# Four mask chunks at once, applied in the transform, and a layer-0 scan without products on GpSimd

## The chip, the cores and the metric

One Trainium2 chip, one of its cores. The metric is the device time of the one launch in microseconds: the median over several runs, and beside it one execution that the hardware profiler recorded. In the profile the engines are PE (TensorE's matmuls), PEld (TensorE's weight loads), DVE (VectorE), ACT (ScalarE), POOL (GpSimd) and SP (SyncE, which here only issues DMAs). POOL also issues DMAs: all gathers by index are issued there.

## The reference

Four samples x of 96 channels and 128 x 128 pixels in float32 go through four layers, each with a group norm `_gn` (32 groups) ahead of it and a residual sum behind it. Cut to what the change touches:

```
x = x + L0(_gn(x))
x = x + L1(_gn(x))
x = x + L2(_gn(x))
x = x + L3(_gn(x))
```

Layer 0 convolves, and then runs a selective scan over the 16,384 pixels, once forward and once backward (K = 2, one state per channel):

```
delta = softplus(dts + dt_proj_b)
dA = exp(delta * A)
dBu = (delta * xs) * Bs
h = dA * h + dBu
ys = h * Cs + Ds * xs
y = ys[forward] + reversed(ys[backward])
y = (y - mean_c(y)) * rsqrt(var_c(y) + 1e-05)
y = y * out_norm_w + out_norm_b
y = y * silu(z)
out = out_proj_w @ y
```

Layer 1 is a mix of spatial, fractional-Fourier and Fourier branches with gates. Layer 2 is a deformable 3 x 3 convolution: an offset for each pixel and tap, a bilinear gather, a weighting, a product with the weights. Layer 3 masks the pixels by their likeness to the centre pixel, takes a two-dimensional cosine transform, runs a scan in each quadrant, and transforms back:

```
center = x[:, :, H // 2, W // 2]
sim = sum_c(x * center) / (|center| * |x| + 1e-06)
x = x * (sim >= 0.7)
xd = Mh @ x @ Mw^T
...
return Mh^T @ (xd + scans) @ Mw
```

## The kernel before

**Tiles.** A plane of 96 channels x 16,384 pixels lies in device memory. Most work is done in NCH = 32 chunks of [96 channels, 512 pixels]. The transforms work in 24 pieces of [128 rows, 4 channels, 128 columns]. In layer 2 a row of the image is 128 pixels on partitions: per tap one gather of [128, 4 x 96] values (tile l_g; 1,152 gathers per sample), then four weighings by bilinear weights (two on ACT, two scalar_tensor_tensor on DVE, tiles l_sm and l_part), a sum, transposes on PE (l_pt), a copy (l_sT), and the product with the layer's weights (l_pc).

**Stages of one sample.** `front` (L635) runs layer 0 (L645), layer 1 (L822) and the offsets of layer 2 (L1212). `back` (L1375) runs the gather of layer 2 (L1386), `layer3_head` (L1493, the mask), and `transform` (L1565, the forward cosine transform). `layer3` (L1604) runs the four quadrant scans, and `inverse` (L1579) the transform back with the residual.

**Lanes.** The front of sample b+1 and the back of sample b are issued as two lanes of one program, and the inverse of sample b-1 runs inside that front, beside layer 0's convolution. So: the front of sample 0 alone, three mixed epochs, each followed by `layer3` of one sample alone, then the back of sample 3 beside the inverse of sample 2, `layer3` of sample 3, and the last inverse. The change touches nothing of `layer3`.

**The order.** Every instruction of both lanes is recorded (class `Program`, L237) and issued by a list scheduler (`issue`, L388). It gives each operation a cost from a table (`cost`, L359) and a due time: `measure` (L282) plans each lane by itself, and the time between two starts is stretched by `pace`, which the code of a stage can set. Each lane's due times are scaled to the same span, so that both lanes end together. An operation that is ready and has the earliest due time goes first. For a DMA the cost table has two numbers, the time on its issuing engine and its share of a common DMA resource ("landing"). The scan of layer 0 sets the pace to 0.1 (L724); layer 1 sets it back to 1. The engines then run their queues strictly in that order. Since all instructions pass through one helper, the profile puts nearly all of them on L65 and SP's DMAs on L412; groups are told apart by tile names.

**Layer 0's scan** (`scan(k, n)`, L728 to L818): 64 calls per sample, k = 0 forward and k = 1 backward. Loads of l_uc (and, in the second half, l_x, l_z and l_part); pd on PE; |.|, relu, exp, ln on ACT; dl = relu + ln on DVE; pB on PE; dA = exp on ACT; du = uc * pB on DVE, then du = du * dl on POOL; the scan h on DVE; its last column copied by ACT (l_e) as the start of the next call; pC on PE; h = h * pC in place on DVE. In the first half of each direction h goes to memory as part_d. In the second half both directions are summed and centred by three matmuls into pm; ACT squares and copies it (l_ct); cavg gives the variance; ct is multiplied by the inverse root on DVE, scaled and shifted by ACT (Identity with v[7] and v[8]), multiplied by sz on DVE, projected (po) and added to l_x.

**The mask** (`layer3_head`). The square of the reference's division is avoided: with q = 0.49 |center|^2, the mask is sqrt(q |x|^2) + 0.7e-6 <= x . center. Each of 32 chunks: load l_hx, normalise on DVE, square on ACT, two 96-column matmuls (pn: |x|^2 by a matrix of ones, pd: by the centre repeated in 96 columns), Sqrt on ACT, comparison on DVE, product with the normalised chunk on POOL, store of 192 KB to m_d. A float32 matmul appears in the profile as two passes.

**The transform** (`transform2`, L1536). Each of 24 pieces: load from m_d as [128, 4, 128], four matmuls (p1), copy on ACT, four matmuls (p2), copy on DVE (l_xo), store to xd_d. `inverse` uses the same function.

**Buffers.** In mixed epochs the back has two PSUM buffers of tag "t" and one of tag "pc"; alone it has five of "t" (`room`, L1378).

Of the kernel before, what the change touches and what calls it, by code (L numbers as in the profile page):

```python
# [236 lines left out]
class Program:  # L237
# [121 lines left out]
    def cost(self, engine, name, out, ins):  # L359
# [5 lines left out]
        if name == "indirect_dma_start":  # L365
            return 1.25, 0.3
# [145 lines left out]
class Net:  # L512
# [132 lines left out]
    def layer0(self, xin, T, beside):  # L645
# [3 lines left out]
        with self.program.pool(name="l0w", bufs=1) as wp, self.program.pool(name="l0p", bufs=1, space=PSUM) as ps:  # L649
# [74 lines left out]
            self.program.pace = 0.1  # L724
            with self.program.pool(name="l0b", bufs=3) as wb:
                edges = [None, None]

                def scan(k, n):  # L728
# [16 lines left out]
                    tmp = wb.tile([C, CH], F32, name="l0_tmp", tag="tmp")  # L745
# [14 lines left out]
                    nc.gpsimd.tensor_tensor(du, du, dl, ALU.mult)  # L760
                    yield
                    h = wb.tile([C, CH], F32, name="l0_h", tag="h", bufs=5)
                    prev = edges[k]
                    if k == 0:
                        nc.vector.tensor_tensor_scan(
                            h, dA, du, 0.0 if prev is None else prev, ALU.mult, ALU.add
                        )
                        edge = h[:, CH - 1 : CH]
                    else:
                        nc.vector.tensor_tensor_scan(  # L770
                            h[:, ::-1], dA[:, ::-1], du[:, ::-1],
                            0.0 if prev is None else prev, ALU.mult, ALU.add,
                        )
                        edge = h[:, 0:1]
                    edges[k] = wb.tile([C, 1], F32, name="l0_e", tag="edge", bufs=6)
                    nc.scalar.copy(edges[k], edge)
# [5 lines left out]
                    nc.vector.tensor_tensor(h, h, pC, ALU.mult)  # L782
                    if not second:
                        nc.sync.dma_start(out=part_d[:, s], in_=h)
                        yield
                        return
# [6 lines left out]
                    nc.tensor.matmul(out=pm, lhsT=center[:, 0, :], rhs=h, start=False, stop=True)  # L793
# [4 lines left out]
                    nc.scalar.copy(ct, pm)  # L798
# [9 lines left out]
                    nc.scalar.activation(ct, ct, AF.Identity, bias=v[:, 8:9], scale=v[:, 7:8])  # L808
                    yield
                    nc.vector.tensor_tensor(ct, ct, sz, ALU.mult)  # L810
# [564 lines left out]
    def back(self, T, alone=False):  # L1375
# [3 lines left out]
        with self.program.pool("l2v", 1) as wp, self.program.pool("l2b", 2) as wb, self.program.pool(  # L1379
            "l2q", room[0], PSUM  # L1380
        ) as ps:
            yield from self.gather(T, wp, wb, ps, *room[1:])
            yield from self.layer3_head(T, wp, wb, ps)
            yield from self.transform(T, wp, wb, ps)

    def gather(self, T, wp, wb, ps, rows, sums, kept, lag, slack):  # L1386
# [60 lines left out]
        def finish(p, c):  # L1447
            g, h = divmod(p, 2)
            w, v = work[g], units.pop((p, c))
            if h == 0 and c == 0:  # L1450
                w.pc = ps.tile([C, CH], F32, name="l2_pc", tag="pc", bufs=1)
# [41 lines left out]
    def layer3_head(self, T, wp, wb, ps):  # L1493

        nc = self.nc
        T.m = self.plane("m_d")
# [4 lines left out]
        cc = wp.tile([C, C], F32, name="l3_cc")  # L1501
        nc.vector.tensor_copy(cc, xm.to_broadcast([C, C]))
        cs = wp.tile([C, 2], F32, name="l3_cs")
        nc.scalar.activation(cs[:, 0:1], xm, AF.Square)
        yield
        pn = ps.tile([128, CH], F32, name="l3_pn", tag="t")
        nc.tensor.matmul(out=pn[:C, 0:1], lhsT=self.ones, rhs=cs[:, 0:1], start=True, stop=True)
        nc.vector.tensor_scalar_mul(cs[:, 1:2], pn[:C, 0:1], 0.49)
        yield

        def piece(t):
            s = slice(t * CH, (t + 1) * CH)
            x = wb.tile([C, CH], F32, name="l3_hx", tag="hx", bufs=5)
            nc.sync.dma_start(out=x, in_=T.x3[:, s])
            yield
            yield
            nc.vector.tensor_scalar(x, x, scale, shift, ALU.mult, ALU.add)
            sq = wb.tile([C, CH], F32, name="l3_sq", tag="sq", bufs=3)
            nc.scalar.activation(sq, x, AF.Square)
            yield  # L1520
            pn = ps.tile([C, CH], F32, name="l3_pn", tag="t")
            nc.tensor.matmul(out=pn, lhsT=self.ones, rhs=sq, start=True, stop=True)
            pd = ps.tile([C, CH], F32, name="l3_pd", tag="t")
            nc.tensor.matmul(out=pd, lhsT=cc, rhs=x, start=True, stop=True)
            yield
            nc.scalar.activation(sq, pn, AF.Sqrt, scale=cs[:, 1:2])
            yield
            nc.vector.scalar_tensor_tensor(sq, sq, 0.7e-6, pd, ALU.add, ALU.is_le)
            yield
            nc.gpsimd.tensor_tensor(x, x, sq, ALU.mult)  # L1530
            nc.sync.dma_start(out=T.m[:, s], in_=x)
            yield

        yield from staggered((piece(t) for t in range(NCH)), 2)

    def transform2(self, src, mat, ps, wt, tags, extra, done):  # L1536
# [4 lines left out]
        def piece(cb):  # L1541
            cs = slice(4 * cb, 4 * cb + 4)
            xt = wt.tile([128, 4, W], F32, name="t2_in", tag=tags[0][0], bufs=tags[0][1])
            nc.sync.dma_start(out=xt, in_=s3[:, cs, :])
            more = extra(cs)
# [10 lines left out]
            p2 = ps.tile([128, 4, 128], F32, name="t2_p2", tag=tags[3], bufs=tags[4])  # L1556
# [8 lines left out]
    def transform(self, T, wp, wb, ps):  # L1565
# [10 lines left out]
        tags = ("hx", 5), ("sq", 3), "t", "t", None  # L1576
        yield from self.transform2(T.m, dctT, ps, wb, tags, lambda cs: None, put)

    def inverse(self, T, out, ps, wt):  # L1579
# [17 lines left out]
        tags = ("in", 4), ("mid", 2), "c", "c", 2  # L1597
# [787 lines left out]
```

## Time and profile before

| what | us |
|---|---|
| median of 3 runs (15122.8 to 15134.95) | 15123.15 |
| profiled execution, its own time | 15123.18 |
| its span, first to last instruction | 15121.3 |
| front of sample 0 alone | 0 to 1304 |
| mixed epochs: gather of the first to end of the last, lengths | 2110, 2135, 2130 |
| four layer-3 scans (first to last matmul l_py), each | 1404 to 1408 |
| last back: gathers | 11949.5 to 13414.2 |
| last back: mask (l_hx), transform (l_xo) | 13429 to 13511, 13527 to 13592 |

The mean granted TensorE clock is 0.898 of full speed. Two lines of the page's busy tenths in 40 slices (each digit is a slice of 378 us; 9 is 90% or more) show that PE and DVE change places as the fuller engine:

```profile
PE   7897887879997978888999688888999744459998
DVE  3626686668998587677999578666999765548997
```

The stretches in which both lines stand at 8 and 9 are the layer-3 scans. Between them lie the mixed epochs, with PE mostly at 7 to 8 and DVE at 5 to 8: there no engine is full all the time, and a stretch has to be read by itself. A time there is read from a table of windows (busy time of each engine between two points), and the cost of one instruction from the groups (mean ns after the comma).

### The profile page before, as it was taken

The page shows a single profiled execution, that of the slowest core. Times are in us where ns is not written, and L with a number is a line of the kernel's source. Part 1 is how long each engine was busy: PE and PEld are TensorE (multiplying, and loading weights), DVE is VectorE, ACT ScalarE, POOL GpSimd, SP SyncE. Part 2 cuts the span into 40 slices and gives each one's busy share as a digit, 9 for nine tenths or more (in the row PEclk, how much of TensorE's full clock was granted, in tenths as well). Part 3 has the DMA queues.
Part 4 walks back from the last instruction along what each step waited for, and adds up shares of the span by engine and source line. Part 5 has one row for each costly group of instructions (what it writes and reads, how often), then busy time and mean ns, then how long its engine had stood idle before and what let it go on. Part 6 is the DMA issues. An engine that isn't in the chain of part 4 may idle for free. (4 is left out here: it accounts for less than half of the span.)

```text
span 15121.3 us, 175326 instructions
## 1 busy us (share of the span) xinstructions
PE 12434.4 (82%) x48096; PEld 5808.6 (38%) x48096; DVE 11294.8 (75%) x21519; ACT 8958.7 (59%) x21605; POOL 10394.8 (69%) x7936
## 2 busy tenths in 40 slices
PE   7897887879997978888999688888999744459998
PEld 3353334343332334444333233534333422233334
DVE  3626686668998587677999578666999765548997
ACT  3614685556664576555666467555666465546664
POOL 2104747748998765765999674773999877748997
PEclk9997898989998989989999899998999855579999
DMA  4546659766666767876666765976666755556666
GB/s 115 143 127 201 191 167 253 229 201 183 187 197 193 234 181 213 239 218 185 194 189 194 218 208 167 259 227 192 194 188 194 216 171 165 167 149 181 189 197 192
DMA packets 1326732, 2914.81 MB, mean 193 GB/s; under 512 B 282864, under 2 KB 768944, under 8 KB 1211440
## 3 DMA queue, kind: packets, MB, share of 16 engines
q1 hardware_dynamic: 1027376, 1997.21, 45.8%
q0 software_dynamic: 298368, 906.38, 20.2%
q8 instruction: 382, 6.26, 0.2%
q14 instruction: 606, 4.96, 0.1%
HBM read 2455.28 MB, written 447.48 MB: 192 GB/s over the span
## 5 line engine op out<-in xcount | busy, mean ns | idle before, releaser
L65 POOL DMA_INDIRECT l_g<-quad_d,l_i x4608 | 4648.1, 1009 | 2541.0 <-issue 1319.5
L65 POOL TENSOR_TENSOR l_hc<-l_h,l_cl 128x1024 f32<-128x1024 f32 x1536 | 3609.7, 2362 | 287.9 <-DVE l_h L65 259.0
L65 PE MATMUL l_py<-l_hc,ident 128*128 128x512 f32 x6144 | 3068.4, 610 | 185.9 <-POOL l_hc L65 182.4
L65 DVE TENSOR_TENSOR_SCAN l_h<-l_dA,l_carry,l_dB 128x512 f32<-128x512 f32 x2304 | 2863.6, 1266 | 1.7
L65 DVE SCALAR_TENSOR_TENSOR l_sm<-l_g,l_v,l_sm 128x96 f32<-128x96 f32 x4608 | 1491.3, 324 | 1137.8 <-ACT l_sm L65 1041.2
L65 ACT ACTIVATE l_dA<-l_dl,l_al 128x512 f32<-128x512 f32 x2304 | 1637.4, 718 | 1111.6 <-DVE l_h L65 1102.3
L65 ACT ACTIVATE l_sm<-l_g,l_v 128x96 f32<-128x96 f32 x4608 | 1677.6, 369 | 731.2 <-DMA l_g<-quad_d,l_i 634.4
L65 ACT ACTIVATE l_part<-l_g,l_v 128x96 f32<-128x96 f32 x4608 | 1654.8, 363 | 234.9 <-DVE l_sm L65 234.4
L65 PEld LDWEIGHTS l_py<-l_hc,ident 128*128 128x128 f32 x6144 | 1133.6, 192 | 1352.9 <-issue 829.2
L65 PE MATMUL l_pc<-l_sT,l_wk 128*96 128x256 f32 (+1 forms) x3584 | 1244.2, 471 | 418.8 <-ACT l_sT L65 418.1
L65 PE MATMUL l_pt<-ident,l_sm 128*128 128x128 f32 (+1 forms) x3584 | 798.3, 327 | 909.4 <-DVE l_sm L65 827.9
L65 DVE TENSOR_TENSOR l_dB<-l_du,l_pB 128x512 f32<-128x512 f32 x2304 | 1493.9, 678 | 49.5 <-POOL l_du L65 26.7
L65 DVE SCALAR_TENSOR_TENSOR l_part<-l_g,l_v,l_part 128x96 f32<-128x96 f32 x4608 | 1485.8, 323 | 36.3 <-ACT l_part L65 35.6
L65 PE MATMUL l_pB<-l_bc,pick 128*128 128x512 f32 x2304 | 1399.8, 635 | 135.4 <-DVE l_dB L65 121.5
L65 POOL TENSOR_TENSOR l_dP<-l_du,l_cl 128x512 f32<-128x512 f32 x768 | 978.6, 1274 | 101.0 <-DMA l_cl<-bc_d 74.6
L65 PEld LDWEIGHTS l_pt<-ident,l_sm 128*128 128x128 f32 (+1 forms) x3584 | 522.9, 165 | 1317.5 <-DVE l_sm L65 922.1
L65 DVE TENSOR_TENSOR_SCAN l_h<-l_dQ,l_carry,l_dP 128x512 f32<-128x512 f32 x768 | 971.8, 1265 | 58.3 <-POOL l_dP L65 54.9
L65 PEld LDWEIGHTS l_pc<-l_sT,l_wk 128*96 128x96 f32 (+1 forms) x3584 | 646.5, 200 | 944.3 <-ACT l_sT L65 513.2
L65 PE MATMUL l_pc<-rows,l_wc 96*32 96x508 f32 (+3 forms) x6912 | 919.6, 601 | 2.4 <-DVE rows L65 2.4
L65 POOL TENSOR_TENSOR l_du<-l_du,l_dl 96x512 f32<-96x512 f32 x256 | 339.6, 1327 | 834.1 <-DVE l_dl L65 487.1
L65 ACT COPY l_sT<-l_pt 128x512 f32<-128x512 f32 (+1 forms) x1024 | 520.8, 522 | 656.1 <-PE l_pt L65 654.0
L65 PE MATMUL l_p<-rows,l_c 96*32 96x508 f32 (+3 forms) x6912 | 823.1, 598 | 83.9 <-issue 46.7
(265 smaller groups left out, 19771.8 us busy)
## 6 DMA issues: line engine op xcount, KB each, us to landing
l_cl<-bc_d SPq DMA_DIRECT2D x512, 1280.0 KB
l_cl<-bc_d SPq DMA_DIRECT2D x512, 640.0 KB
quad_d<-l_qt SPq DMA_DIRECT2D x124, 768.0 KB
l_g<-quad_d,l_i POOLq DMA_INDIRECT x4608
x<-l_x SPq DMA_DIRECT2D x352, 192.0 KB
l_uc<-u_d SPq DMA_DIRECT2D x256, 192.0 KB
l_x<-x SPq DMA_DIRECT2D x224, 192.0 KB
l_xs<-x SPq DMA_DIRECT2D x116, 256.0 KB
```

The lines of the kernel that those rows point to most:

```text
L65: ins = op(*args, **kw).ins
```

## The change

1. The scheduler's cost table gives a gather a landing of 0.66 instead of 0.3, and the scan of layer 0 a pace of 0.3 instead of 0.1.
2. Layer 0's scan: du * dl on DVE instead of POOL; the copy of the last column falls away, since h is no longer overwritten (the product goes to a tile l_y) and the next call reads h's last column; h has four buffers instead of five, tmp two instead of three; the copy of pm applies the scale v[7], the Identity operation falls away, and the shift v[8] is added in the product with sz (scalar_tensor_tensor).
3. The mask: groups of four chunks. Each chunk's two matmuls have 32 output columns at partitions 32j to 32j+31 of shared PSUM tiles, so that one Sqrt and one comparison serve four chunks at [128, 512]. One row of each 32 is stored (2 KB) to mask_d, which is loaded once as a [128, 128] image. pd has the "pc" buffer. Small tiles give scale and shift as rows (by_channel) for the transform's layout.
4. The transform loads x3 instead of m_d, and normalises each of four channels on DVE ([128, 128]) and masks the piece on POOL ([128, 512], the mask broadcast). p2 has the "pc" buffer in mixed epochs.

```diff
@@ -363,7 +363,7 @@
...
         if name == "indirect_dma_start":
-            return 1.25, 0.3
+            return 1.25, 0.66
         if engine == "PE":
@@ -721,7 +721,7 @@
...
-            self.program.pace = 0.1
+            self.program.pace = .3
             with self.program.pool(name="l0b", bufs=3) as wb:
@@ -742,7 +742,7 @@
...
                     dl = wb.tile([C, CH], F32, name="l0_dl", tag="dl")
-                    tmp = wb.tile([C, CH], F32, name="l0_tmp", tag="tmp")
+                    tmp = wb.tile([C, CH], F32, name="l0_tmp", tag="tmp", bufs=2)
                     bias = v[:, 1 + k : 2 + k]
@@ -757,31 +757,30 @@
...
                     yield
-                    nc.gpsimd.tensor_tensor(du, du, dl, ALU.mult)
-                    yield
-                    h = wb.tile([C, CH], F32, name="l0_h", tag="h", bufs=5)
+                    nc.vector.tensor_tensor(du, du, dl, ALU.mult)
+                    yield
+                    h = wb.tile([C, CH], F32, name="l0_h", tag="h", bufs=4)
                     prev = edges[k]
...
                         )
-                        edge = h[:, CH - 1 : CH]
+                        edges[k] = h[:, CH - 1 : CH]
                     else:
...
                         )
-                        edge = h[:, 0:1]
-                    edges[k] = wb.tile([C, 1], F32, name="l0_e", tag="edge", bufs=6)
-                    nc.scalar.copy(edges[k], edge)
+                        edges[k] = h[:, 0:1]
                     if second:
...
                     yield
-                    nc.vector.tensor_tensor(h, h, pC, ALU.mult)
+                    y = wb.tile([C, CH], F32, name="l0_y", tag="y")
+                    nc.vector.tensor_tensor(y, h, pC, ALU.mult)
                     if not second:
-                        nc.sync.dma_start(out=part_d[:, s], in_=h)
+                        nc.sync.dma_start(out=part_d[:, s], in_=y)
                         yield
@@ -790,12 +789,12 @@
...
                     nc.tensor.matmul(out=pm, lhsT=center[:, 0, :], rhs=part, start=False, stop=False)
-                    nc.tensor.matmul(out=pm, lhsT=center[:, 0, :], rhs=h, start=False, stop=True)
+                    nc.tensor.matmul(out=pm, lhsT=center[:, 0, :], rhs=y, start=False, stop=True)
                     yield
...
                     nc.scalar.activation(sq, pm, AF.Square)
-                    nc.scalar.copy(ct, pm)
+                    nc.scalar.activation(ct, pm, AF.Copy, scale=v[:, 7:8])
                     yield
@@ -805,9 +804,7 @@
...
                     yield
-                    nc.scalar.activation(ct, ct, AF.Identity, bias=v[:, 8:9], scale=v[:, 7:8])
-                    yield
-                    nc.vector.tensor_tensor(ct, ct, sz, ALU.mult)
+                    nc.vector.scalar_tensor_tensor(ct, ct, v[:, 8:9], sz, ALU.add, ALU.mult)
                     yield
@@ -1380,8 +1377,8 @@
...
             yield from self.gather(T, wp, wb, ps, *room[1:])
-            yield from self.layer3_head(T, wp, wb, ps)
-            yield from self.transform(T, wp, wb, ps)
+            yield from self.layer3_head(T, wp, wb, ps, room[2])
+            yield from self.transform(T, wp, wb, ps, alone)
@@ -1448,7 +1445,7 @@
...
             if h == 0 and c == 0:
-                w.pc = ps.tile([C, CH], F32, name="l2_pc", tag="pc", bufs=1)
+                w.pc = ps.tile([128, CH], F32, name="l2_pc", tag="pc", bufs=1)[:C]
             for i, k in enumerate(v.ks):
@@ -1490,50 +1487,64 @@
...
-    def layer3_head(self, T, wp, wb, ps):
+    def layer3_head(self, T, wp, wb, ps, sums):
         nc = self.nc
-        T.m = self.plane("m_d")
+        mask_d = self.plane("mask_d", (NCH // 4, 4 * CH))
         mid = (H // 2) * W + W // 2
...
         nc.vector.tensor_scalar(xm, xm, scale, shift, ALU.mult, ALU.add)
-        cc = wp.tile([C, C], F32, name="l3_cc")
-        nc.vector.tensor_copy(cc, xm.to_broadcast([C, C]))
-        cs = wp.tile([C, 2], F32, name="l3_cs")
-        nc.scalar.activation(cs[:, 0:1], xm, AF.Square)
+        cc = wp.tile([C, 32], F32, name="l3_cc")
+        nc.vector.tensor_copy(cc, xm.to_broadcast([C, 32]))
+        cs = wp.tile([128, 2], F32, name="l3_cs")
+        nc.scalar.activation(cs[:C, 0:1], xm, AF.Square)
+        wide = wb.tile([C, 4, 128], F32, name="l3_wide", tag="hx", bufs=5)
+        for k, v in enumerate((scale, shift)):
+            nc.vector.tensor_copy(wide[:, k, :], v.to_broadcast([C, 128]))
+        nc.vector.memset(wide[:, 2, :], 1.0)
         yield
         pn = ps.tile([128, CH], F32, name="l3_pn", tag="t")
-        nc.tensor.matmul(out=pn[:C, 0:1], lhsT=self.ones, rhs=cs[:, 0:1], start=True, stop=True)
-        nc.vector.tensor_scalar_mul(cs[:, 1:2], pn[:C, 0:1], 0.49)
+        nc.tensor.matmul(out=pn[:, 0:1], lhsT=wide[:, 2, :], rhs=cs[:C, 0:1], start=True, stop=True)
+        nc.vector.tensor_scalar_mul(cs[:, 1:2], pn[:, 0:1], 0.49)
+        pq = ps.tile([128, CH], F32, name="l3_pq", tag="t")
+        for k in range(2):
+            nc.tensor.matmul(
+                out=pq[:, C * k : C * k + C], lhsT=wide[:, k, :], rhs=self.ident[:C, :C], start=True, stop=True
+            )
+        keep = wb.tile([128, 9, C], F32, name="l3_keep", tag="sm", bufs=sums).rearrange("p k c -> p (k c)")
+        T.by_channel, T.mask = keep[:, : 2 * C], keep[:, 2 * C : 2 * C + W]
+        nc.vector.tensor_copy(T.by_channel, pq[:, : 2 * C])
         yield
-        def piece(t):
-            s = slice(t * CH, (t + 1) * CH)
-            x = wb.tile([C, CH], F32, name="l3_hx", tag="hx", bufs=5)
-            nc.sync.dma_start(out=x, in_=T.x3[:, s])
-            yield
-            yield
-            nc.vector.tensor_scalar(x, x, scale, shift, ALU.mult, ALU.add)
-            sq = wb.tile([C, CH], F32, name="l3_sq", tag="sq", bufs=3)
-            nc.scalar.activation(sq, x, AF.Square)
-            yield
-            pn = ps.tile([C, CH], F32, name="l3_pn", tag="t")
-            nc.tensor.matmul(out=pn, lhsT=self.ones, rhs=sq, start=True, stop=True)
-            pd = ps.tile([C, CH], F32, name="l3_pd", tag="t")
-            nc.tensor.matmul(out=pd, lhsT=cc, rhs=x, start=True, stop=True)
-            yield
-            nc.scalar.activation(sq, pn, AF.Sqrt, scale=cs[:, 1:2])
-            yield
-            nc.vector.scalar_tensor_tensor(sq, sq, 0.7e-6, pd, ALU.add, ALU.is_le)
-            yield
-            nc.gpsimd.tensor_tensor(x, x, sq, ALU.mult)
-            nc.sync.dma_start(out=T.m[:, s], in_=x)
-            yield
-        yield from staggered((piece(t) for t in range(NCH)), 2)
-    def transform2(self, src, mat, ps, wt, tags, extra, done):
+        def group(g):
+            pn = ps.tile([128, CH], F32, name="l3_pn", tag="t")
+            pd = ps.tile([128, CH], F32, name="l3_pd", tag="pc", bufs=1)
+            for j in range(4):
+                x = wb.tile([C, CH], F32, name="l3_hx", tag="hx", bufs=5)
+                nc.sync.dma_start(out=x, in_=T.x3[:, (4 * g + j) * CH : (4 * g + j + 1) * CH])
+                yield
+                nc.vector.tensor_scalar(x, x, scale, shift, ALU.mult, ALU.add)
+                sq = wb.tile([C, CH], F32, name="l3_sq", tag="sq", bufs=3)
+                nc.scalar.activation(sq, x, AF.Square)
+                at = slice(32 * j, 32 * j + 32)
+                nc.tensor.matmul(out=pn[at], lhsT=self.ones[:, :32], rhs=sq, start=True, stop=True)
+                nc.tensor.matmul(out=pd[at], lhsT=cc, rhs=x, start=True, stop=True)
+                yield
+            m = wb.tile([128, CH], F32, name="l3_m", tag="l2_x", bufs=3)
+            nc.scalar.activation(m, pn, AF.Sqrt, scale=cs[:, 1:2])
+            nc.vector.scalar_tensor_tensor(m, m, 0.7e-6, pd, ALU.add, ALU.is_le)
+            for j in range(4):
+                nc.sync.dma_start(
+                    out=mask_d[g : g + 1, j * CH : (j + 1) * CH], in_=m[32 * j : 32 * j + 1]
+                )
+            yield
+        for g in range(NCH // 4):
+            yield from group(g)
+        nc.sync.dma_start(out=T.mask, in_=mask_d.rearrange("g (r w) -> (g r) w", w=W))
+    def transform2(self, src, mat, ps, wt, tags, extra, done, prepare=None):
@@ -1542,6 +1553,8 @@
...
             nc.sync.dma_start(out=xt, in_=s3[:, cs, :])
+            if prepare is not None:
+                prepare(cs, xt)
             more = extra(cs)
@@ -1553,7 +1566,7 @@
...
             yield
-            p2 = ps.tile([128, 4, 128], F32, name="t2_p2", tag=tags[3], bufs=tags[4])
+            p2 = ps.tile([128, 4, 128], F32, name="t2_p2", tag=tags[3], bufs=tags[5])
             for j in range(4):
@@ -1562,7 +1575,7 @@
...
-    def transform(self, T, wp, wb, ps):
+    def transform(self, T, wp, wb, ps, alone):
@@ -1573,8 +1586,15 @@
...
-        tags = ("hx", 5), ("sq", 3), "t", "t", None
-        yield from self.transform2(T.m, dctT, ps, wb, tags, lambda cs: None, put)
+        def prepare(cs, xt):
+            for j in range(4):
+                scale = T.by_channel[:, cs.start + j : cs.start + j + 1]
+                shift = T.by_channel[:, C + cs.start + j : C + cs.start + j + 1]
+                nc.vector.tensor_scalar(xt[:, j, :], xt[:, j, :], scale, shift, ALU.mult, ALU.add)
+            nc.gpsimd.tensor_tensor(xt, xt, T.mask.unsqueeze(1).to_broadcast([128, 4, W]), ALU.mult)
+        tags = ("hx", 5), ("sq", 3), "t", *(("t", None, None) if alone else ("pc", None, 1))
+        yield from self.transform2(T.x3, dctT, ps, wb, tags, lambda cs: None, put, prepare)
@@ -1594,7 +1614,7 @@
...
-        tags = ("in", 4), ("mid", 2), "c", "c", 2
+        tags = ("in", 4), ("mid", 2), "c", "c", 2, 2
         yield from self.transform2(T.yd_d, dct, ps, wt, tags, take, put_out)
```

## The prediction

> **What bounds the kernel now.** First the busy shares, which name no engine:
>
> ```profile
> PE 12434.4 (82%) x48096; PEld 5808.6 (38%) x48096; DVE 11294.8 (75%) x21519; ACT 8958.7 (59%) x21605; POOL 10394.8 (69%) x7936
> ```
>
> So the span must be cut into stages, by the first and last instruction of tiles that only one stage has. It falls into the front of sample 0 alone (0 to 1304 us), three mixed epochs of about 2120 us (back of one sample beside the front of the next), the last back alone (11949 to 13628), and four layer-3 scans of about 1405 us, whose code does not change. Second, the table by stretch. Rows one to five are the second mixed epoch (layer 0's convolution, its scan, layer 1, the last convolution, the offsets with mask and transform); six is the first half of sample 0's scan; seven and eight are mask and transform of the last back. Columns: stretch, length, busy time of PE, weight load, DVE, ACT, POOL, granted clock, DMA share, GB/s.
>
> ```profile
> 4848.00:5358.00 510.00, 409.17 (x2836) 183.38 (x2837) 277.63 (x863) 267.27 (x838) 365.88 (x367) 0.89 0.82 242
> 5358.00:5815.00 457.00, 381.83 (x921) 147.88 (x919) 416.26 (x721) 385.63 (x870) 238.48 (x196) 0.92 0.52 157
> 5815.00:6259.00 444.00, 362.60 (x1657) 235.37 (x1658) 292.34 (x936) 245.38 (x810) 308.99 (x303) 0.88 0.92 252
> 6259.00:6542.00 283.00, 269.14 (x2012) 101.09 (x2011) 172.70 (x545) 143.19 (x486) 211.81 (x215) 0.97 0.76 224
> 6542.00:6971.00 429.00, 341.40 (x1408) 196.19 (x1406) 306.25 (x826) 247.10 (x659) 177.76 (x164) 0.85 0.67 207
> 268.00:430.00 162.00, 133.94 (x279) 44.03 (x280) 136.86 (x168) 134.61 (x258) 52.08 (x39) 0.96 0.36 107
> ```
> ```profile
> 13429.00:13521.00 92.00, 70.78 (x130) 22.52 (x130) 42.56 (x67) 39.52 (x65) 44.76 (x32) 0.85 0.44 129
> 13521.00:13628.00 107.00, 75.33 (x437) 55.22 (x437) 24.49 (x56) 29.02 (x47) 3.21 (x4) 0.89 0.55 148
> ```
>
> Each stage has another limit: the scan DVE (416 of 457 us, 91%), layer 1 the DMA engines (0.92), the last convolution PE (95%), the fifth stretch PE (80%) with DVE close (71%). Third, the groups of instructions inside the scan stage (mean after the comma), and of the whole page the convolution with 32 output columns:
>
> ```profile
> L65 POOL DMA_INDIRECT l_g<-quad_d,l_i x132 | 153.2, 1160 | 82.0 <-issue 31.4 <-DVE l_sm L65 30.0 <-ACT l_dl L65 10.1
> L65 POOL TENSOR_TENSOR l_du<-l_du,l_dl 96x512 f32<-96x512 f32 x64 | 85.8, 1342 | 136.8 <-DVE l_dl L65 110.5 <-DVE l_du L65 25.6
> L65 DVE SCALAR_TENSOR_TENSOR l_sm<-l_g,l_v,l_sm 128x96 f32<-128x96 f32 x137 | 60.0, 444 | 6.9 <-ACT l_sm L65 6.2 <-DMA l_g<-quad_d,l_i 0.5
> L65 DVE TENSOR_TENSOR l_dl<-l_dl,l_tmp 96x512 f32<-96x512 f32 x64 | 56.7, 888 | 2.7 <-ACT l_tmp L65 2.3
> L65 DVE TENSOR_TENSOR l_h<-l_h,l_pC 96x512 f32<-96x512 f32 x64 | 43.1, 674 | 1.1 <-ACT l_e L65 0.7 <-PE l_pC L65 0.3
> L65 ACT ACTIVATE l_ct<-l_ct,l_v 96x512 f32<-96x512 f32 x32 | 26.0, 811 | 13.4 <-DVE l_ct L65 13.3
> ```
> ```profile
> L65 PE MATMUL l_pc<-rows,l_wc 96*32 96x508 f32 (+3 forms) x6912 | 919.6, 601 | 2.4 <-DVE rows L65 2.4
> ```
>
> To be seen: l_dl and l_sm take 888 and 444 ns here, though the median of l_sm in the same stage is 308 and an l_dl that meets no POOL product takes about 682. DVE is held up by POOL's own product.
>
> **The change, part by part.** The sum starts from the profiled execution: 15123.18 us, 1.9 over its span and within 0.1 of the 15123.15 median.
>
> *Where gathers go.* The planner's two new numbers (landing 0.66, pace 0.3) add no instruction; they only reorder. The compiled order of both kernels shows how many weighing operations (two per gather) stand on DVE beside each front stage, per mixed epoch: convolution 688 to 694, scan 274 to 324, layer 1 603 to 678, last convolution 413 to 383, offsets 326 to 225. So +3, +25, +37, -15 and -50 gathers.
>
> *Scan, mixed epochs.* DVE gets 64 products that were POOL's. An added one is like l_h<-l_h,l_pC, 0.674 us: +43 us. What they stop doing to DVE: 137 x (444-308) + 137 x (423-308) = 34 us on l_sm and l_part, and 64 x (888-682) = 13 on l_dl; the instructions that truly overlap a POOL product carry 30 and 14, and I take 44. The last product of the gate becomes a scalar_tensor_tensor, 32 x (0.740-0.674) = +2. The 25 gathers bring 25 x 2 x 0.308 = 15 and their share of the final additions, 25/4.57 x 0.683 = 4. DVE: 416+43-44+2+19 = 436. At today's 91% that is 479 us, at 95% it is 459; I take 465, +8 (0 to +23), since the chain loses a step. It loses POOL's 1.34 us and its wait (137 us idle), the edge copy (64 x 0.184 on ACT) and the affine (32 x 0.811): ACT falls by 38 and regains 25 x 2 x 0.365 = 18. Next in the chain l_h then waits for DVE's own queue. POOL falls from 238 to 238-86+25x1.05 = 179, so its queue has room. The fourth h buffer and second tmp buffer cost nothing while DVE sets the pace. If the 44 us do not come back, the stage goes to (436+44)/0.91 = 527.
>
> The Trainium skill, "SBUF — State Buffer" (section "SBUF: two separate sides"), says a DVE operation with two SBUF inputs and GpSimd lock each other out of a shared port for a whole instruction. The row: gathers here take 1160 ns on average, median 1050, against 967 in the last back. By the rule 64 new two-input products would block POOL for up to 43 us per epoch; by the row the excess over the quiet stretch is 0.19 us each; either way POOL at 179 of 465 us hides it, so it enters no sum.
>
> *Scan, sample 0 alone.* First half: DVE is 137 of 162 us; 32 products add 21.6 and the quieter l_dl (1.09 to 0.68 us here) gives back 13: +8 against a removed POOL step. Second half: PE is busy in 169.7 of 170 us, which covers everything. I take 0 (-5 to +10).
>
> *Layer 1, mixed.* 37 more gathers. A gather's share of the DMA engines is 0.202 x 15121/4608 = 0.66 us; at 0.92 busy, +27. Bounds: PE cost alone (transposes and products, (798.3+1244.2)/4608 = 0.44 us each by the page's l_pt and l_pc groups) +16; POOL's whole 1.2 us, +45.
>
> *Convolutions, mixed.* +3 gathers x 0.66/0.82 = +2. In the last, 15 fewer x 0.44/0.95 = -7 (0 to -14).
>
> *Mask, transform and offsets, mixed (fifth stretch).* PE loses 50 x 0.44 = 22 us, and the mask's 128 passes at 0.63 us become 128 passes of 32 columns. The convolution row shows what four neighbours on different columns do: 919.6/6912 = 0.13 us each of elapsed time, though one lasts 0.60. Here the order mixes pd and pn of one chunk (same columns), so I take half of 78 us, -37. PE: 341 to 282; at 80% that is 354 us, -75. DVE loses 50 x 2 x 0.308 + 8 of gathers, 24 x 0.68 of comparisons, and gains 96 tensor_scalars of 128x128, no row; nearest are a 96x96 copy, 0.205, and 128x96 weighing, 0.308; I take 0.28: +27. DVE: 306-39-16+27 = 278, at 71% 390 us, -39. POOL loses 32 x 1.4 = 45 and gains 24 masked products of 512 columns at about 1.35, 32. I take -50 (-20 to -75), between the two.
>
> SP's queue changes: 32 stores of 192 KB go, 32 stores of one row (2 KB) and one load come, 0.30 us of issue each, so SP is even; 6.3 MB of writes per sample vanish. What waits behind a mask store on SP is the load of the next group's chunks, at most one Sqrt and one comparison (1.4 us).
>
> Per mixed epoch: +2+8+27-7-50 = -20; three give -60.
>
> *Last back alone.* The mask's 32 chunks take 92 us, PE 71: two products of two passes each, 2.78 of 2.84 us per chunk. After, per group of four: 16 passes between 0.13 (2.1 us) and 0.63 (10 us), I take 0.32, 5.2; then Sqrt 0.68 and comparison 0.68 before pd's single buffer is free, and 0.5 for handoffs (estimated from the 0.1 to 0.2 us between dependent instructions): 7 us. Eight groups 56, the new small tiles +3: -33 (-50 to +0). The turn to the transform stays a store that must land before a load (5.3 us from the last m_d issue to the first product now). The transform keeps its loop of two products and a copy, 2.78 us a piece; its new work (4 x 0.28 + 1.35 on DVE and POOL) lies ahead of it under five buffers, costing nothing; without that cover 24 x 2.5 = 60 us.
>
> The skill speaks against the 2 KB stores: "DMA: Bandwidth & Descriptors", Rules for kernel authors, wants small transfers coalesced, and "Anatomy of one DMA — SWDGE (gpsimd) path" puts about 2 us fixed on each. By that the last four stores cost an estimated 2 us once; if nothing overlapped, 64 us. The trace has no such store.
>
> Total: 0 - 60 - 33 = -93: **15,030 us**.
>
> **Rivals.**
> *Larger gain.* PE is the true limit of the epoch: fifth stretch -75, last convolution -14, layer 1 only +16, scan 0, convolution +2: -71 x 3 - 50 = -263, 14,860. For: PE leads in four of five rows. Against: DVE at 91% and DMA at 0.92 exactly where gathers are added.
> *Nothing.* The gathers are only moved: what the offsets lose, scan and layer 1 take (fifth stretch -39, scan +23, layer 1 +27, -5: +6 x 3), the last head alone gains 33: 15,108; with a head that saves only 10, 15,131. For: each moved gather costs about the same in either place.
> *Slower: the scan's DVE gets no relief.* If gathers, which also slow DVE's operations, keep l_sm and l_dl long, the stage is 527 us, +70: per epoch +2+70+27-7-50 = +42, x 3 - 33 = +93, 15,216. It decides from +39 on that stage (496 us). For: DVE is already at 91%. Against: l_sm's median of 308 with gathers running all along.
> *Not what it says:* the scan might get no more gathers; the order shows 274 to 324, so I give that nothing.
>
> **How the numbers follow.** Forecast 0.46, larger gain 0.20, nothing 0.17, slower 0.17. A measurement tells 0.2% (30 us) from no change. Nearly all of the first two is below 15,093: faster 0.66, same 0.17, slower 0.17. The forecast's own range is 14,950 to 15,095. To hold 8 in 10 I leave out the lower end of the larger gain (0.09) and the upper end of the slower case (0.11): 14,880 to 15,190.
>
> **What would show it.** In after's scan stage l_dl near 0.68 and l_sm near 0.31 us, DVE above 91%, the stage 457 to 480 us; layer 1 about 470 at DMA 0.92 or more; the fifth stretch near 380; the last mask near 59 us with 32-column passes overlapping; transform 67. Wrong if l_sm stays above 0.4, or if a mask group takes 10 us, or if the transform waits for DVE or POOL.

## The result, and the profile after

The changed kernel takes 15220.18 us (median of 6 runs, 15186.34 to 15243.47), the kernel before beside it 15122.97: a ratio of 1.0065, 95% interval 1.0051 to 1.0079. It is slower by about 97 us where 93 us less was forecast. The profiled execution took 15215.73 us, its span is 15213.7.

The busy shares of the changed kernel, first line of its page:

```profile
PE 12702.1 (83%) x48112; PEld 5786.9 (38%) x48112; DVE 11312.4 (74%) x22079; ACT 8797.0 (58%) x21125; POOL 10025.4 (66%) x7648
```

PE is busy for 268 us more, though the mask's matmuls became cheaper. Where that lies, the table by stretch tells: the second mixed epoch again (layer 0's convolution, scan, layer 1, last convolution, and offsets with mask and transform), then mask and transform of the last back. Columns as in the prediction: stretch, length, busy time of PE, weight load, DVE, ACT, POOL, clock, DMA share, GB/s.

```profile
4838.00:5372.00 534.00, 471.43 (x2846) 185.41 (x2847) 282.46 (x872) 272.67 (x848) 369.57 (x372) 0.93 0.79 232
5372.00:5815.00 443.00, 381.78 (x959) 152.33 (x957) 423.11 (x843) 375.32 (x834) 171.59 (x158) 0.93 0.59 174
5815.00:6310.00 495.00, 362.96 (x1699) 243.89 (x1702) 312.42 (x1018) 272.19 (x903) 362.07 (x348) 0.86 0.88 244
6310.00:6663.00 353.00, 346.93 (x1987) 108.77 (x1979) 166.86 (x521) 131.03 (x443) 193.42 (x194) 0.99 0.58 170
6663.00:7029.00 366.00, 309.03 (x1350) 174.67 (x1348) 273.55 (x778) 198.14 (x517) 113.94 (x104) 0.85 0.63 198
...
13562.00:13605.00 43.00, 35.34 (x134) 10.91 (x134) 21.95 (x50) 23.62 (x40) 0.00 (x0) 0.92 0.45 139
13605.00:13720.00 115.00, 77.63 (x439) 56.81 (x436) 54.09 (x149) 29.29 (x47) 33.59 (x28) 0.87 0.50 137
```

Against the rows of before: +24, -14, +51, +70, -63. The last convolution is the surprise. It has fewer gathers beside it than before (194 instead of 215), fewer instructions on PE (1987 instead of 2012), and PE is busy for 347 us instead of 269, in 98% of the stretch. The three mixed epochs take 2107, 2199 and 2207 us instead of 2110, 2135 and 2130, and the last back 1637 instead of 1678: -3, +64, +77 and -41, together the +97. (The first epoch's last convolution also gets 94 us longer, but what follows it there gets 118 shorter.)

Two groups of the changed kernel's page say which instructions of PE became dear: l_pc<-rows,l_wc is layer 0's convolution, l_p<-rows,l_c the last one. Both are 3 x 3 convolutions, and each of the nine positions (a tap) is four matmuls with 32 output columns, eight passes. The third line is l_p before (the other stands in the prediction):

```profile
L65 PE MATMUL l_p<-rows,l_c 96*32 96x508 f32 (+3 forms) x6912 | 1058.7, 598 | 49.0 <-DMA rows<-cat_d 43.7
...
L65 PE MATMUL l_pc<-rows,l_wc 96*32 96x508 f32 (+2 forms) x6912 | 1038.3, 595 | 2.7 <-DVE rows L65 2.7
```
```profile
L65 PE MATMUL l_p<-rows,l_c 96*32 96x508 f32 (+3 forms) x6912 | 823.1, 598 | 83.9 <-issue 46.7
```

One pass lasts about 598 ns before and after. The elapsed time that all of them cover, the number after the bar, rises from 823.1 + 919.6 = 1743 us to 1058.7 + 1038.3 = 2097. They overlap less. The timeline of PE in the last convolution shows why (start, length, engine, instruction, how many in a row). First the kernel before, then the changed one:

```profile
6381.82 1.04 PE L65 MATMUL l_p<-rows,l_c 96*32 96x512 f32 x8
6382.80 0.76 PE L65 MATMUL l_pt<-ident,l_sm 128*128 128x128 f32 x5
6383.49 1.90 PE L65 MATMUL l_p<-rows,l_c 96*32 96x508 f32 x13
```
```profile
6453.32 1.04 PE L65 MATMUL l_p<-rows,l_c 96*32 96x512 f32 x2
6454.30 0.67 PE L65 MATMUL l_pc<-l_sT,l_wk 128*96 128x256 f32 x2
6454.90 1.04 PE L65 MATMUL l_p<-rows,l_c 96*32 96x508 f32 x2
6455.87 0.44 PE L65 MATMUL l_pt<-ident,l_sm 128*128 128x128 f32 x2
6456.24 1.04 PE L65 MATMUL l_p<-rows,l_c 96*32 96x508 f32 x2
```

Eight passes, the four matmuls of a tap on their four groups of columns, take 1.04 us together. Two passes, one matmul of the four, take 1.04 us alone. In both traces the unbroken runs of l_p take (medians) 1.04 to 1.06 us for 2 to 8 passes, 1.90 to 1.92 for 10 to 16, 2.75 to 2.78 for 18 to 24 and 3.60 to 3.62 for 26 to 32: about 0.2 us per run and 0.85 for every eight passes begun. The changed order puts transposes (l_pt) and products (l_pc<-l_sT,l_wk) of the gather lane between the four. Such a break stands within a tap 258 times before and 603 times after, in the compiled orders and in the traces alike (the expectations call breaks "broken taps"; they fall on 246 and 381 of the 1,728 taps; l_pz of layer 0, also 32 columns wide, isn't counted). That is 354 us more for 345 more breaks, 1.03 us each.

### The profile page after: what moved, and what is told of

Its sections match the earlier page's. It is cut to its first block, busy times and chain, and to the rows that moved or that the text cites. A ratio compares the mean times of both kernels' runs of the same rounds, so it can differ in the third digit from the quotient of the medians.

```text
span 15213.7 us, 174518 instructions
## 1 busy us (share of the span) xinstructions
PE 12702.1 (83%) x48112; PEld 5786.9 (38%) x48112; DVE 11312.4 (74%) x22079; ACT 8797.0 (58%) x21125; POOL 10025.4 (66%) x7648
## 5 line engine op out<-in xcount | busy, mean ns | idle before, releaser
L65 DVE SCALAR_TENSOR_TENSOR l_sm<-l_g,l_v,l_sm 128x96 f32<-128x96 f32 x4608 | 1426.5, 313 | 1283.3 <-ACT l_sm L65 1238.4
L65 ACT ACTIVATE l_sm<-l_g,l_v 128x96 f32<-128x96 f32 x4608 | 1619.5, 369 | 782.4 <-DMA l_g<-quad_d,l_i 699.1
L65 ACT ACTIVATE l_part<-l_g,l_v 128x96 f32<-128x96 f32 x4608 | 1607.9, 364 | 415.1 <-DVE l_sm L65 412.4
L65 DVE SCALAR_TENSOR_TENSOR l_part<-l_g,l_v,l_part 128x96 f32<-128x96 f32 x4608 | 1430.6, 314 | 169.0 <-ACT l_part L65 168.7
L65 PE MATMUL l_p<-rows,l_c 96*32 96x508 f32 (+3 forms) x6912 | 1058.7, 598 | 49.0 <-DMA rows<-cat_d 43.7
L65 PE MATMUL l_pc<-rows,l_wc 96*32 96x508 f32 (+2 forms) x6912 | 1038.3, 595 | 2.7 <-DVE rows L65 2.7
L65 PEld LDWEIGHTS l_pB<-l_bc,pick 128*128 128x128 f32 x2304 | 437.9, 190 | 1062.6 <-DVE l_dB L65 839.7
```

The lines of the kernel that those rows point to most:

```text
L65: ins = op(*args, **kw).ins
```

## The experiments

**Four runs for three theories.** A: the broken taps cost the time. B: layer 1 is held by the DMA engines and got more gathers. C (the forecast's rival): DVE gets no relief in the scan. The kernel before took 15143.33 us (13 runs) beside these.

The first undoes one number:

```diff
-            return 1.25, 0.66
+            return 1.25, 0.3
```

> The changed kernel with one number undone: a gather's landing in the scheduler's table is 0.3 again instead of 0.66. Theory A (broken taps): the changed order puts gather products of the other lane between the four 32-column matmuls of a convolution tap, 603 times against 258 before, and the elapsed PE time of these matmuls rose from 1743 to 2097 us, about 1.03 us for each break. This kernel's order has 293 breaks: up to 310 x 1.03 = 319 us less, so 14900 to 14980 us, and the last convolution of a mixed epoch back from 353 to about 285 us. Theory B (layer 1 is held by DMA and given more gathers): here layer 1 gets 601 weighings instead of 678, and only its 51 us per epoch come back: 15070 to 15130, last convolution still near 350. Theory C (the scan's DVE gets no relief): no change, 15220.

Measured: 14861.31 us, ratio 0.9813 (0.9797 to 0.9829), a little below A's range. The landing number alone is worth 2.5% of the time. Layer 1 and the last convolution of its second mixed epoch:

```profile
5689.00:6126.00 437.00, 355.42 (x1648) 235.55 (x1650) 288.98 (x931) 243.64 (x802) 307.06 (x299) 0.89 0.93 252
6126.00:6405.00 279.00, 266.20 (x2014) 100.25 (x2007) 171.69 (x541) 141.47 (x483) 211.46 (x214) 0.97 0.78 228
```

Both came back, so A and B are not told apart yet; C is out. The second keeps the landing of 0.66 and only forbids broken taps:

```diff
+        op.narrow = name == "matmul" and out.rows[1] - out.rows[0] <= 32 and out.at[0].size > 256
...
-                starts.append((start, op.key + late, op.lane, len(starts), op))
+                first = 1.0 if op.narrow and self.quad % 4 else 0.0
+                starts.append((start, op.key + late - first, op.lane, len(starts), op))
...
+            self.quad += op.narrow
```

> The changed kernel with landing 0.66 as it is, and one rule more in the scheduler: once the first of four 32-column matmuls is issued on PE, the other three go ahead of anything else. The order has 0 breaks and gives the stages the same gathers as the changed kernel (338, 679, 378 and 225 weighings in scan, layer 1, last convolution and offsets of the second mixed epoch, against 324, 678, 383 and 225). Theory A: up to 603 x 1.03 = 621 us less PE time, of which DVE and DMA will let only a part through; 14700 to 14950, the last convolution at 270 us or less. Theory B: layer 1 keeps its 679 weighings, so 15180 or more. Theory C: no change, 15220.

Measured: 14897.53 us, ratio 0.9835 (0.9818 to 0.9851). The same two stretches:

```profile
5717.00:6210.00 493.00, 368.14 (x1713) 247.39 (x1717) 314.62 (x1019) 271.99 (x903) 356.59 (x343) 0.86 0.88 243
6210.00:6475.00 265.00, 254.48 (x1981) 99.14 (x1974) 166.19 (x517) 130.89 (x443) 183.89 (x182) 0.98 0.74 216
```

The last convolution falls from 353 to 265 us and layer 0's convolution from 534 to 497, while layer 1 stays at 493. With the gathers in nearly the same places the rule alone is worth 2.3% (ratio 0.9835 against 1.0065): A is what made the kernel slow. The rule also holds for the mask's 32-column matmuls, but the last back's mask takes 43 us with it and without it. B's stretch is longer too, but 51 us there stand against 63 us less in the offsets.

The third puts the landing of 0.66 alone into the kernel before; the edit is the first one reversed.

> The kernel before with one number changed: landing 0.66. No instruction differs. Breaks 258 to 460. Theory A: up to 202 x 1.03 = 208 us more, 15220 to 15330, with the last convolution above 330 us. Theory B: 670 weighings in layer 1 instead of 603 cost about 50 us per epoch there, and the last convolution stays near 285: about 15200 or less, if the offsets give back. Theory C: no change, 15123.

Measured: 15338.64 us, ratio 1.0129 (1.0112 to 1.0146), just above A's range. No instruction differs from before, and:

```profile
5834.00:6326.00 492.00, 365.65 (x1690) 244.33 (x1694) 311.19 (x1008) 270.19 (x900) 350.72 (x336) 0.87 0.89 239
6326.00:6713.00 387.00, 376.65 (x2049) 108.63 (x2042) 186.02 (x576) 144.95 (x489) 225.83 (x227) 0.98 0.61 173
```

Layer 1 gets 48 us longer, the last convolution 104. The fourth puts the rule of the second into the kernel before.

> The kernel before with the rule that keeps the four 32-column matmuls of a tap together: 0 breaks instead of 258, gathers where they were (284, 603, 413, 326). Theory A: up to 258 x 1.03 = 266 us less, 14880 to 15030. Theories B and C: no change, 15123.

Measured: 15118.7 us, ratio 0.9986 (0.9976 to 0.9996). Here A's number missed twice. 258 breaks are gone and only 135 us of elapsed time with them (1743 to 1608), 0.52 us per break: counted in the traces, the runs of l_p begin 916 groups of eight passes before and 864 with the rule, 52 fewer for 115 broken taps (in the changed kernel they begin 1,131). And the run gains 0.14%. The last convolution, and POOL in it:

```profile
6256.00:6540.00 284.00, 255.39 (x2013) 99.01 (x2012) 172.02 (x545) 142.89 (x486) 213.65 (x216) 0.95 0.76 224
```
```profile
L65 POOL DMA_INDIRECT l_g<-quad_d,l_i x216 | 213.9, 990 | 72.8 <-issue 60.3 <-DVE l_part L65 6.9 <-DMA l_g<-quad_d,l_i 4.6
```

PE lost 14 us and the stretch none, since POOL fills it: 213.9 us of gathers and 60.3 of "issue", time in which POOL waits for nothing that the profile shows, are 274 of 284 us. A gather takes POOL about 1.3 us, though it shows as 0.99 busy. Alone, in the last back, 1,152 of them take 1465 us, 1.27 each. So a break would cost only where PE and not POOL is the limit; the eighth run tests that.

**Four runs for the parts.** The kernel before took 15129.44 us (7 runs) beside them. The fifth has the scan's part alone, the sixth mask and transform alone, both with the scheduler's old numbers; the seventh has both parts with the old numbers:

```diff
-            return 1.25, 0.66
+            return 1.25, 0.3
...
-            self.program.pace = .3
+            self.program.pace = 0.1
```

> The kernel before with the scan's part of the change alone (product on DVE, no edge copy, affine folded into the product), the scheduler's numbers, mask and transform as before; 248 broken taps. If the prediction's relief is right, the scan stage of a mixed epoch goes from 457 to about 440 us and sample 0's scan from 371 to 367, no other stage moves: 15045 to 15090. Rival (the whole gain of the first experiment of 282 us sits in mask and transform): 15110 to 15140, scan still near 457.

Measured: 15041.1 us, ratio 0.9941 (0.9924 to 0.9958). The scan's stretch of the second epoch, with 274 weighings as before:

```profile
5323.00:5745.00 422.00, 367.80 (x916) 141.79 (x914) 403.70 (x784) 357.83 (x765) 142.52 (x132) 0.95 0.58 170
```

It falls by 35 us, more than the 17 expected, and the run ends 4 us below the first range: DVE has 12 us less to do in spite of 64 more products, and is busy for 96% instead of 91%. The rival is out.

> The kernel before with the mask and transform of the change alone, scan and scheduler's numbers as before; 263 broken taps. If mask and transform carry what the prediction said: last back -40, the fifth stretch of each mixed epoch -30 to -50: 14950 to 15000. Rival (in mixed epochs the mask's gain is only filled with gathers from elsewhere): the last back's -40 alone, 15070 to 15100.

Measured: 15015.34 us, ratio 0.9919 (0.9902 to 0.9935). The last back takes 1639 us instead of 1678; the mixed epochs 2066, 2131 and 2117 instead of 2110, 2135 and 2130. The first theory asked for too much, the rival for too little.

> The changed kernel with both of the scheduler's numbers as before (landing 0.3, pace 0.1): scan part and mask part together, 263 broken taps. If pace 0.3 is worth nothing by itself, the time of the first experiment, 14860 +-20. If pace 0.3 is what lets the scan's room be used (341 or 313 weighings in the scan against 232 here), 14890 to 14960.

Measured: 14934.7 us, ratio 0.9868 (0.9849 to 0.9887): the two parts add up (88 + 114 of 195 us). The second outcome held: pace 0.3 (first experiment) gains another 73 us by the two medians, 87 if each is set against the kernel before beside it. In the second epoch it moves 40 gathers to the scan, which gets 24 us longer (394 to 418, first l_pd to last l_x), and the offsets lose 62 (423 to 361, first offset product to last l_xo).

The eighth joins the first two edits: the changed kernel with landing 0.3 and the rule for taps.

> The changed kernel with landing 0.3 and with the rule that keeps the four matmuls of a tap together: 0 broken taps instead of 293. Theory A as first stated (each break costs 1.03 us on the path): 14560 to 14650. Theory A as the fourth experiment left it (breaks cost only where PE is the limit; with gathers placed as before, POOL's rate of one gather in 1.3 us holds the stages): 14810 to 14861.

Measured: 14819.21 us, ratio 0.9794 (0.9777 to 0.981), the fastest of the study, 2.1% under the kernel before. The second of the two forms of A held. Against the first experiment the gain is small and the intervals overlap. Against the second, which differs in the landing alone, it is 0.4% (0.9794 against 0.9835): with the taps kept together, that is all that a landing of 0.66 costs.

**What a gather costs in each place.** The ninth is the changed kernel with landing 0.8. For it, the tenth and the eleventh the kernel before took 16779.28 us, 11% more than in the other runs, so that only ratios can be read, and they don't compare well with the others: gathers were slower there (see the last section).

```diff
-            return 1.25, 0.66
+            return 1.25, 0.8
```

> The changed kernel with landing 0.8 instead of 0.66. The order has 234 broken taps (fewer than the kernel before), but puts far more gathers beside the scan (476 weighings in the second mixed epoch against 324 in the changed kernel and 313 at landing 0.3) and layer 1 (807 against 678 and 601), and hardly any beside the last convolution (62). If broken taps alone set the time: 14820 to 14880, as at landing 0.3. If the place of the gathers has a price too: against landing 0.3 the scan +65 (81 gathers at 0.8 us of DVE), layer 1 +76 (103 at 0.66 / 0.9 of the DMA engines), layer 0's convolution +21, the last convolution -88 (it can't go under the 190 us that it takes in sample 0 alone), offsets -20: +54 per mixed epoch, 15020 (14960 to 15080).

Measured: ratio 1.0127 (1.0096 to 1.0158), above both outcomes (about 0.98 and 0.99). With fewer breaks than before the kernel is slower: here the place of the gathers has a price.

> The kernel of the eighth experiment (landing 0.3, the four matmuls of a tap together) with pace 0.4 in the scan: 366 weighings beside it instead of 323. If the gain of pace 0.3 over 0.1 (74 us between the seventh and the first experiment) goes on: 14780 to 14810. If DVE, at 95% in the scan, is full: 14820 to 14860, the scan longer by 43 x 0.5 x 0.8 = 17 us per epoch.

> The same with pace 0.2: 291 weighings beside the scan. If more gathers beside the scan are a gain: 14830 to 14870. If the optimum lies below 0.3: under 14819.

Measured: 0.9822 (0.98 to 0.9844) and 0.983 (0.9802 to 0.9859). These two can't be told apart, and the eighth (pace 0.3) had no run beside them; where the best pace lies stays open. The twelfth is the eighth with landing 0.8 (kernel before 15119.18):

> The kernel of the eighth experiment (the four matmuls of a tap together, 0 broken taps) with landing 0.8 instead of 0.3. Beside it 435 weighings stand at the scan, 811 at layer 1 and 98 at the last convolution of the second mixed epoch, against 323, 601 and 402. If only broken taps matter: the ratio to the kernel before of the eighth experiment, 0.979 (14820 us on a chip where the kernel before takes 15130). If the place of the gathers has a price of its own: 56 more gathers beside the scan at 0.8 us of DVE (+45), 105 more beside layer 1 at 0.66 / 0.9 (+77), the last convolution down to 190 at best (-84), offsets -25 and layer 0's convolution +15: +28 to +60 per mixed epoch, ratio 0.984 to 0.993.

Measured: 15132.93 us, ratio 1.0012 (1.0003 to 1.0022); more than either outcome allowed. Scan, layer 1 and last convolution, first of the eighth, then of the twelfth:

```profile
5230.00:5666.00 436.00, 380.65 (x961) 149.31 (x959) 420.31 (x843) 376.43 (x833) 164.92 (x152) 0.94 0.60 175
5666.00:6099.00 433.00, 357.19 (x1649) 235.69 (x1651) 289.09 (x931) 244.10 (x803) 308.23 (x298) 0.88 0.93 255
6099.00:6373.00 274.00, 248.71 (x2000) 95.19 (x1993) 169.57 (x532) 137.87 (x471) 207.08 (x211) 0.96 0.77 229
```
```profile
5317.00:5834.00 517.00, 410.35 (x1038) 168.65 (x1036) 465.48 (x971) 412.86 (x947) 256.48 (x234) 0.89 0.60 180
5834.00:6410.00 576.00, 418.94 (x1826) 272.93 (x1830) 359.79 (x1170) 324.71 (x1066) 427.34 (x416) 0.81 0.84 235
6410.00:6617.00 207.00, 200.54 (x1757) 101.90 (x1750) 77.13 (x200) 37.04 (x126) 50.29 (x51) 0.98 0.49 140
```

By the count of weighings 105 more gathers in layer 1 cost 143 us, 1.36 each (POOL issues 118 more there: 1.21 each), and the DMA share falls from 0.93 to 0.84 as they come: layer 1 isn't held by the DMA engines. POOL's gathers in layer 1 in the kernel before, the changed kernel and the twelfth:

```profile
L65 POOL DMA_INDIRECT l_g<-quad_d,l_i x303 | 309.0, 1020 | 132.7 <-issue 102.5 <-DVE l_part L65 18.0 <-DMA l_g<-quad_d,l_i 10.3
L65 POOL DMA_INDIRECT l_g<-quad_d,l_i x348 | 362.2, 1041 | 129.6 <-issue 95.7 <-ACT sp_tb L65 14.8 <-DVE l_part L65 9.8
L65 POOL DMA_INDIRECT l_g<-quad_d,l_i x416 | 427.5, 1028 | 148.0 <-issue 117.3 <-ACT l_sm L65 13.3 <-DMA l_g<-quad_d,l_i 9.7
```

Gathers and "issue" fill 412 of 444 us, 458 of 495 and 545 of 576: layer 1 goes at POOL's rate (1.47, 1.42 and 1.38 us per gather). Beside the scan 56 more by the count of weighings (82 issued) cost 81 us, 1.45 (0.99) each; which engine sets that price isn't shown. 152 fewer beside the last convolution save 67 us, 0.44 each, of which PE's busy time accounts for 48; in the 207 us that are left PE is busy for 97% and POOL for 24%, so that with few gathers PE is the limit there.

## Why the prediction was wrong

**The step that failed** is in the paragraph on where gathers go: "The planner's two new numbers (landing 0.66, pace 0.3) add no instruction; they only reorder." The order was read for how many gathers stand in each stage, and not for what stands between neighbours. So the last convolution was put at -7 us and layer 0's convolution at +2; they measured +70 and +24. The number that warned was in the prediction itself: 0.13 us of elapsed time for a matmul that lasts 0.60 holds only while four of them stand together. Used for the mask, it was not applied to the instructions it was taken from. Of the 88 us by which the second epoch missed its -20 (measured +68), the last convolution has 77 and layer 0's convolution 22; layer 1 adds 24, and the scan and the fifth stretch give back 22 and 13. Undoing the landing alone gives 14861 us, and forbidding broken taps alone 14898.

**Layer 1** was put at +27 (16 to 45), because of a DMA share of 0.92. It measured +51. A high share was taken for the limit; the twelfth experiment adds gathers there and the share falls. The stretch goes at POOL's rate of a gather: of the 51 us, POOL's gathers with their issue time account for 46 (412 to 458). The term's upper bound took 1.2 us a gather for POOL; the stretch goes at 1.4.

**The scan** was right in its mechanism. The groups of the changed kernel's scan stage (mean after the comma):

```profile
L65 POOL DMA_INDIRECT l_g<-quad_d,l_i x158 | 173.1, 1096 | 271.7 <-ACT l_dl L65 105.5 <-ACT l_sm L65 46.3 <-issue 44.4
...
L65 DVE SCALAR_TENSOR_TENSOR l_sm<-l_g,l_v,l_sm 128x96 f32<-128x96 f32 x162 | 49.7, 307 | 0.3 <-ACT l_sm L65 0.3
...
L65 DVE TENSOR_TENSOR l_du<-l_du,l_dl 96x512 f32<-96x512 f32 x64 | 43.7, 682 | 0.7
L65 DVE TENSOR_TENSOR l_dl<-l_dl,l_tmp 96x512 f32<-96x512 f32 x64 | 43.4, 678 | 2.1 <-ACT l_tmp L65 2.1
```

l_dl took 678 ns (0.68 forecast), l_sm 307 (0.31). The size was off on the good side: -14 us instead of +8, with DVE at 96% (95% had been the upper value). The relief was put at 44 us; the fifth experiment, with as many gathers as before, shows about 58 (12 us less on DVE in spite of 44 for the products and 2 for the gate). Why so little idle time is left on DVE is not shown by a run of its own. The port rule of the Trainium skill ("SBUF — State Buffer", section "SBUF: two separate sides") sets a DVE operation with two SBUF inputs only against a GpSimd operation that reads SBUF. POOL's own product was one, and l_dl and l_sm got shorter when it went; the prediction counted a gather as one too, which no run shows. Gathers took 1096 ns here against 1160 before, with 64 more such products on DVE, so the sum was right to leave a block out. Sample 0's scan measured 351 us against 355 (first l_pd to last l_x), within the -5 to +10.

**Mask, transform and offsets** in the mixed epoch: -63 (forecast -50, -20 to -75). **The last back**: -41 (forecast -33). A mask group took 5.1 us (41 for eight), not 7; the transform kept its time, 67 us from its first to its last output against 65, with its DVE and POOL work hidden as said. The last 2 KB store is issued at 13607.8 us and the load of the mask, which waits for it, at 13609.4: 1.6 us, where the prediction estimated 2. The transform's first product follows 4.8 us behind that store's issue, against 5.2 before. The other stores left no mark that the trace shows. In the sum of the fifth stretch half of 78 us is put at 37 instead of 39, which changes nothing.

**The rivals.** "Slower: the scan's DVE gets no relief" gave 15,216 us, which is the measured time by coincidence; its mechanism did not happen: the scan's part alone made that stretch 35 us shorter. Without the planner's landing the change comes to the number of the larger gain: 14861 us, 282 below the kernel before beside it. That is a coincidence too. What that rival named, PE as the true limit of the whole epoch, is not shown by the runs: the fourth experiment took 124 us of busy time from PE and gained 0.14%.

The parts, each run set against the kernel before beside it: scan -88, mask and transform -114 (together -195), pace 0.3 another -87, landing 0.66 +379. The last two are differences between successive runs, so their sum of +97 proves nothing by itself; what it rests on are the runs.

Left open: why the scheduler breaks taps at a landing of 0.66. In the compiled orders (0.4 to 0.6 were not run) the changed kernel has 293 breaks at 0.3, 306 at 0.4, 416 at 0.5, 591 at 0.6 and 234 at 0.8, and, at 0.66, 554 to 606 when one lane's due times are moved by 3% either way. So a small shift between the lanes doesn't explain it.

## What to carry to other kernels

Where matmuls on different column groups overlap, the order within the group of four is part of the cost: cut the compiled order into unbroken runs, and price each run by the groups of four that it begins (here 0.85 us each and 0.2 per run), not by its matmuls. That is time on PE; it is time of the kernel only in stretches that PE holds. A change of a scheduler's number is a change of every stage, and is to be costed as such. Before a stage is called bound by the fullest engine, divide its length by the number of slow issues (here gathers) in it: a like quotient in several stages (here 1.3 to 1.5 us) points to the issuing engine, even where its busy share is 75%.

## What the runs showed of the hardware that was not expected

- POOL's gather of 128 rows has a pace of 1.27 us (1465 us for 1,152 alone) though each shows as 0.97 us busy; the rest stands as idle time with the releaser "issue" (60.3 us for 216 gathers). POOL at 75% busy was full.
- A single 32-column float32 matmul in two passes takes PE 1.04 us, the four of a tap together 1.04 to 1.06; the next four in an unbroken run add 0.85.
- The same gathers can be slower on another occasion: where the kernel before took 16779 us, 1,152 gathers alone took 1719 us instead of 1465 (tenth against eighth experiment), with the layer-3 scans unchanged at 1407 to 1413 us and the front of sample 0, which has no gathers, at 1300. The record names the same chip number for these runs as for the first four, where the kernel before took 15143 us; what differed is not known.
